# A four-layer image kernel: a feed-forward part on 32x32 tiles, a first norm per token, displaced rows of C, separate sign chains and another order of the filters

## The chip, the cores and the metric

The kernel runs on one core of one Trainium2 chip. Its time is device microseconds of one execution; the time before is the median of three executions. One further execution was profiled, and all rows of the profile come from that one.

The engines are named as in the profile: PE (TensorE; PEld its weight loads), DVE (VectorE), ACT (ScalarE), POOL (GpSimd) and SP (SyncE, which in the kernel before issues nearly every DMA; SPq is its queue). Each engine works through its own instructions in order and waits on semaphores for the others.

## The reference

Input and output are float32 images of shape (4, 64, 128, 128). Four layers follow each other:

- Layer 0: a mamba over 16,384 tokens of an image, 64 channels, 128 inner channels, 16 states, then a projection and a normalization.
- Layer 1: a windowed transform, whose windows need the sign function and an inverse of a 128x128 matrix.
- Layer 2: two 3x3 convolutions with batch norms, a gate out of means over shrinking windows, a relu.
- Layer 3: two 3x3 convolutions, then a mamba with 64 states and a feed-forward part with a depthwise 3x3 convolution over 256 hidden channels.

Layer 3 is where most of the change lies. Cut to the core:

```python
y = relu(conv2d(x, conv1_w, conv1_b))
t = tokens(conv2d(y, conv2_w, conv2_b))
t = t + mamba(layernorm(t, ln1_w, ln1_b), ...)
t = t + ffn(layernorm(t, ln2_w, ln2_b), ...)
return x + image(t)

def step(h, inp):              # in the mamba, for each token
    d_t, b_t, c_t, u_t = inp
    h = h * exp(d_t[..., None] * A) + (d_t * u_t)[..., None] * b_t[:, None, :]
    return h, einsum('bdn,bn->bd', h, c_t)

def ffn(t):
    h = t @ fc1_w.T + fc1_b                    # 64 -> 256 channels
    h = conv2d(image(h), dw_w, dw_b, groups=256)
    return gelu(tokens(h)) @ fc2_w.T + fc2_b
```

## The kernel before

The layers run one after the other, each with its own pools; images go through device memory between them. In the profiled span layer 0 lies at 0 to about 3130 us, layer 1 to about 4285, the convolutions of layers 2 and 3 to about 5090, layer 3's mamba to about 16,380 and the feed-forward part to the end.

**The mambas** (`_Mamba`, used by layer 0 and layer 3). Tokens are taken in chunks of 1024; four images of 16,384 tokens make 64 chunks. A chunk is a row of iterations, 16 in layer 0 and 64 in layer 3. An iteration holds 32 of the 128 inner channels with 4 of the states in its 128 partitions, and 1024 tokens in the free dimension; four iterations, one for each 32 channels, make a group of 4 states. ACT makes the decays `da` (L582); PE spreads B or its product over the partitions in PSUM (L514 and L520; of the second kind DVE multiplies `bx` by `du`, L526); DVE's scan (L626) runs the recurrence from `da` and `bx` into a slot of `ring`, written 8 elements after the slot's start; POOL multiplies the slot by the rows of C, `cb`, and writes it to the slot's start (L632); PE sums over the states (`y`, L457). `cb` is loaded by `_C` (L417): SyncE sends four 128 KB transfers for a group, each one row of C broadcast to 32 partitions, into a 128x1024 tile with three buffers, up to 6 iterations ahead. The tile, the slots of `ring` and the operands start at multiples of 16 bytes.

The work of a chunk that isn't an iteration is written as generators, whose steps the loop puts in at given iterations: `ahead` before the chunk (in layer 3 the centring at 41 to 43 iterations before the chunk's start, the causal convolution at 32 before), `behind` after it. The convolution takes four taps as two matmul passes (L300): the tile S holds the normalized tokens in partitions 64 to 127 and the same tokens shifted by one in partitions 0 to 63. Before, the shifted copy is made by loading it: X is read twice from `t3`, once one token earlier, and centring (PE), square and reciprocal root (ACT) and multiply (POOL, L1518) run over 128x1024, so each token is normalized twice. `tail` keeps the last two columns for the next chunk. `behind` (L1524 on) loads the tokens `tr` and the image x3 as `xr`, projects, adds `tr` to `xr` on POOL (L1537), stores the sum in `s3` and the second norm in `n3`.

**Layer 1's sign function** (L939 to L960): two matrices, km plus and minus a small multiple of the identity, go through 27 iterations of X, each X*X, a combination Z with the identity, and X*Z symmetrized. Both matrices lie beside each other in one tile: two matmuls, one DVE operation over 128x256 (L950), four matmuls, one DVE copy over 128x256 (L956). The inversion after it (L966 to L978) has one such chain alone.

**The convolutions of layers 2 and 3** (`layer2_convs3`): first all weights and the vectors of the batch norms are loaded and combined, some thirty small loads; then the first strips are loaded (`fetch`), turned on DVE and POOL (`turned`, L1214; L1218 and L1220 are POOL's two subtractions of image rows) and multiplied (`product`, L1223).

**The feed-forward part** (`layer3_ffn`). 32 strips of 16 rows of 128 pixels. The 256 hidden channels are two halves of 128: half 1 (`h1`) has its nine depthwise taps on DVE (`taps`, L1663 and L1665, each over 128x2048), half 0 (`h0`) on PE as matmuls with 64x64 diagonal matrices (L1717): four tiles at once, two row halves by two column halves, so that a step of nine handles 8 of the 16 rows, and nine steps run twice per strip. `first` is a generator: it loads N with its halo, lets POOL zero the edge columns of `h` (L1629, L1630), and three times per half runs fc1 on PE (L1638) into one PSUM tile `ph`, which ACT evacuates into `h` in two activations (L1643); it is stepped between the taps of the strip before. `second` (L1675) sums fc2 on PE into `po` and lets DVE add bias and `res` (L1684); SyncE then stores `out` (L1690). `res` is loaded by SyncE from `s3` (L1706), which already holds x + t. The DVE taps of the next strip are cut into pieces of 4, 1 and 4 between the adds.

Of the kernel before, what the change touches and what calls it, by code (L numbers as in the profile page):

```python
# [170 lines left out]
class _Mamba:  # L171
# [245 lines left out]
    def _C(self, c, g):  # L417
        t = self.t("cb", 3)
        for q in range(NQ):
            n = NQ * g + q  # L420
            self.nc.sync.dma_start(t[DD * q : DD * (q + 1)], c["C"][n : n + 1, :].to_broadcast([DD, TC]))
        return t
# [423 lines left out]
def _dual_window(tc, K, lm, nscale, r4):  # L846
# [10 lines left out]
    with ExitStack() as ctx:  # L857
# [81 lines left out]
        for a, _ in {*SIGN_STEPS, *INV_STEPS}:  # L939
            eyes[a] = cp.tile([P, 2, P], F32, name=f"eye{a}".replace(".", "_"))  # L940
            nc.vector.tensor_scalar_mul(eyes[a], K.eye.unsqueeze(1).to_broadcast([P, 2, P]), a / 2)
        X = ip.tile([P, 2, P], F32, name="X", tag="X")
        for i, sg in enumerate((tau, -tau)):
            nc.vector.scalar_tensor_tensor(X[:, i, :], K.eye, sg, km, ALU.mult, ALU.add)
        for a, b in SIGN_STEPS:
            py = pp.tile([P, 2, P], F32, name="pk", tag="pk")
            for i in range(2):
                nc.tensor.matmul(py[:, i, :], X[:, i, :], X[:, i, :], start=True, stop=True)
            Z = ip.tile([P, 2, P], F32, name="Z", tag="Z")
            nc.vector.scalar_tensor_tensor(Z, py, -b / 2, eyes[a], ALU.mult, ALU.add)  # L950
            px = pp.tile([P, 2, P], F32, name="pk", tag="pk")
            for i in range(2):
                nc.tensor.matmul(px[:, i, :], X[:, i, :], Z[:, i, :], start=True, stop=False)
                nc.tensor.matmul(px[:, i, :], Z[:, i, :], X[:, i, :], start=False, stop=True)
            X = ip.tile([P, 2, P], F32, name="X", tag="X")
            nc.vector.tensor_copy(X, px)  # L956
        pi, qi = cp.tile([P, P], F32, name="pi"), cp.tile([P, P], F32, name="qi")
        nc.vector.tensor_sub(qi, X[:, 0, :], X[:, 1, :])
# [10 lines left out]
        for a, b in INV_STEPS:  # L969
# [3 lines left out]
            nc.vector.scalar_tensor_tensor(Z, py[:, 0, :], -b / 2, eyes[a][:, 0, :], ALU.mult, ALU.add)  # L973
# [287 lines left out]
def layer2_convs3(ctx, tc, K, w, w3, x2, x3, t3):  # L1261
# [8 lines left out]
    wts = [cv.weights(cp, src, f"cw{k}") for k, src in enumerate((w["c1"], w["c2"], w3["c1"], w3["c2"]))]  # L1270
    eps = cp.tile([P, 1], F32, name="eps2")
    nc.vector.memset(eps, 1e-5)
    norms = []
    for i in "12":
        g, b, m, v, cb = (
            _dup(nc, cp, w[k], f"{k}_") for k in (f"bn{i}_g", f"bn{i}_b", f"bn{i}_m", f"bn{i}_v", f"c{i}_b")
        )
        _rstd(nc, v, v, eps)
        nc.vector.tensor_mul(g, g, v)
        nc.vector.tensor_sub(cb, cb, m)  # L1280
        nc.vector.tensor_mul(cb, cb, g)
        nc.vector.tensor_add(cb, cb, b)
        norms.append((g, cb))
    bias3 = [_dup(nc, cp, w3[k], f"{k}3") for k in ("c1_b", "c2_b")]
    eca = cp.tile([P, 3], F32, name="eca")
    nc.sync.dma_start(eca, w["eca"].to_broadcast([P, 3]))
    band = cp.tile([P, P], F32, name="band")
    nc.vector.tensor_scalar(band, K.sh0, eca[:, 0:1], None, ALU.mult)
    nc.vector.scalar_tensor_tensor(band, K.sh1, eca[:, 1:2], band, ALU.mult, ALU.add)
    nc.vector.scalar_tensor_tensor(band, K.sh2, eca[:, 2:3], band, ALU.mult, ALU.add)  # L1290

# [143 lines left out]
    fetch(2)  # L1435
    V = {0: cv.turned(source(*units[0], got[units[0]]))}
    last = None
    for n, (kind, pr, s) in enumerate(units):
        p = cv.product(V.pop(n), wts[kind])
        fetch(loads.index((kind, pr, s)) + 3 if kind in (0, 2) else 0)  # L1440
        if last is not None and kind == 0 and s == 2:
            gated(last)
            last = None
# [19 lines left out]
def layer3_mamba(ctx, tc, K, w, t3, x3, s3, n3):  # L1463
# [16 lines left out]
    tail = cp.tile([P, 2], F32, name="tail")  # L1480

    def load(c):
        b, t0 = c["at"]
        X = c["X"] = m.t("X", 1)
        if t0:
            nc.sync.dma_start(X[:64], t3[b, :, t0 - 1 : t0 - 1 + TC])
        else:
            nc.gpsimd.memset(X[:64, 0:1], 0.0)
            nc.sync.dma_start(X[:64, 1:], t3[b, :, : TC - 1])
        nc.sync.dma_start(X[64:], t3[b, :, t0 : t0 + TC])  # L1490

    def ahead(c):
# [3 lines left out]
        S = m.t("S", 1, TC + 2)  # L1496
        if t0:
            nc.gpsimd.tensor_copy(S[:, :2], tail)
        else:
            nc.gpsimd.tensor_copy(S[:, :2], pad.to_broadcast([P, 2]))  # L1500
        xs, sq = m.tmp("nxc"), m.tmp("nsq")
        yield m.slot(c, "centre")
        pm = m.take()
# [8 lines left out]
        pm = m.take()  # L1512
# [5 lines left out]
        nc.gpsimd.tensor_mul(S[:, 2:], xs, sq)  # L1518
        if not t0:
            nc.gpsimd.tensor_copy(S[:64, 2:3], pad[:64])  # L1520
        nc.gpsimd.tensor_copy(tail, S[:, TC:])
        yield from m.front(c, S, lambda: None)

    def behind(c, yg):  # L1524
        b, t0 = c["at"]
        tx = m.tmp("tx")
        tr, xr = tx[:, :512], tx[:, 512:]
        for h in range(NH):
            nc.sync.dma_start(tr[64 * h : 64 * (h + 1)], _halves(t3[b], t0)[h])
            nc.sync.dma_start(xr[64 * h : 64 * (h + 1)], _halves(x3[b], t0)[h])  # L1530
# [6 lines left out]
        nc.gpsimd.tensor_add(xr, xr, tr)  # L1537
# [17 lines left out]
        for h in range(NH):  # L1555
            nc.sync.dma_start(_halves(s3[b], t0)[h], xr[64 * h : 64 * (h + 1)])
            nc.sync.dma_start(_halves(n3[b], t0)[h], o[64 * h : 64 * (h + 1)])
# [6 lines left out]
def layer3_ffn(ctx, tc, K, w, n3, s3, out):  # L1564
# [7 lines left out]
    NK = R // 8  # L1572
    half = [slice(64 * h, 64 * (h + 1)) for h in range(2)]
    cp = ctx.enter_context(tc.tile_pool(name="ffc", bufs=1))
    wp = ctx.enter_context(tc.tile_pool(name="ffw", bufs=2))
    hp = ctx.enter_context(tc.tile_pool(name="ffp", bufs=1, space=PSUM))
    dp = ctx.enter_context(tc.tile_pool(name="ffd", bufs=2, space=PSUM))
# [3 lines left out]
    f2 = cp.tile([P, 64], F32, name="f2")  # L1581
    nc.sync.dma_start(f2, w["fc2_wT"][P:, :])

    f2h = cp.tile([P, 2, 64], F32, name="f2h")
    dwb = cp.tile([P, 2], F32, name="dwb")
    dww = cp.tile([P, 2, 9], F32, name="dww")
    diag = cp.tile([P, 9, 64], F32, name="diag")
    for h in range(2):
        nc.sync.dma_start(f1[half[h]], w["fc1_wT"].rearrange("c (t q) -> c t q", t=2))
        nc.sync.dma_start(f2h[half[h]], w["fc2_wT"][:P, :].rearrange("(i q) c -> q i c", i=2))  # L1590
        nc.sync.dma_start(dwb[half[h]], w["dw_b"][:P, :].rearrange("(i q) o -> q (i o)", i=2))
    b1 = cp.tile([P, 2], F32, name="ff_fc1_b")
    nc.sync.dma_start(b1, w["fc1_b"].rearrange("(t q) o -> q (t o)", t=2))

    g, n = (_dup(nc, cp, w[k], f"ff_{k}") for k in ("ln2_w", "ln2_b"))
# [5 lines left out]
    dwb1 = cp.tile([P, 1], F32, name="dwb1")  # L1601
    nc.sync.dma_start(dwb1, w["dw_b"][P:, :])
    nc.sync.dma_start(dww, w["dw_w"].rearrange("(t q) k -> q t k", t=2))
    for k in range(9):
        for h in range(2):
            nc.vector.tensor_scalar(
                diag[half[h], k, :], K.eye[half[h], half[h]], dww[half[h], 0, k : k + 1], None, ALU.mult
            )
    b2 = _dup(nc, cp, w["fc2_b"], "fc2b_")

    def first(b, r0, H):


        nimg = n3[b].rearrange("c (r w) -> c r w", w=WW)
        N = wp.tile([P, HR, WW], F32, name="N", tag="N")
        rng = []
        if r0 == 0:
            nc.vector.memset(N[:64, 0:1, :], 0.0)
        if r0 + R == HH:
            nc.vector.memset(N[64:, HR - 1 : HR, :], 0.0)  # L1620
# [5 lines left out]
        yield  # L1626
# [24 lines left out]
    strips = [(b, r0) for b in range(B) for r0 in range(0, HH, R)]  # L1651
    H = {}
    for _ in first(*strips[0], H):
        pass

    def taps(h1):

        g1 = wp.tile([P, R, WW], F32, name="g1", tag="g1")
        for k in range(9):
# [6 lines left out]
            yield g1  # L1666

    def more(gen, n):
        for _ in range(n):
            g = next(gen, None)  # L1670
        return g

    def second(n, g0, g1, res, o, kk):

        b, r0 = strips[n]  # L1675
        po = op.tile([P, 2, 4, WW], F32, name="po", tag="po")
        for h in range(2):
            r = 8 * kk + 4 * h
            nc.tensor.matmul(po[half[h], h], f2, g1[:, r : r + 4, :], start=True, stop=False)  # L1679
        for i in range(2):  # L1680
            for h in range(2):
                nc.tensor.matmul(po[half[h], h], f2h[half[h], i, :], g0[i][half[h], kk], start=False, stop=i == 1)  # L1682
        for h in range(2):
            nc.vector.scalar_tensor_tensor(  # L1684
                o[half[h], kk], po[half[h], h], b2[half[h]], res[half[h], kk], ALU.add, ALU.add
            )
        if kk == NK - 1:
            oimg = out[b].rearrange("c (r w) -> c r w", w=WW)
            for q in range(R // 4):
                nc.sync.dma_start(oimg[:, r0 + 4 * q : r0 + 4 * q + 4, :], o[half[q % 2], q // 2])  # L1690

    pin = _Pin(tc)
    g1 = more(taps(H[1]), 9)
    rest, owed = iter(()), None
    for n, (b, r0) in enumerate(strips):
# [3 lines left out]
        ahead = first(*strips[n + 1], H) if n + 1 < len(strips) else iter(())  # L1701
        next(ahead, None)

        res = wp.tile([P, NK, 4, WW], F32, name="res3", tag="res3")
        for q in range(R // 4):
# [136 lines left out]
```

## Time and profile before

| | us |
|---|---|
| median of three executions | 17,327.41 (17,321.47 to 17,331.91) |
| profiled execution | 17,333.11 |
| its span | 17,331.3 |
| PE busy in the span | 13,927.6 (80%) |
| DVE | 15,802.2 (91%) |
| ACT | 14,324.0 (83%) |
| POOL | 14,169.2 (82%) |
| mean granted TensorE clock | 0.909 |

Busy shares are means over stages with different limits, so each stage has to be read by itself. A row of the groups names the line, the engine, the operation, output and input tiles with their partitions and elements, the count, then busy time and mean ns of one, then the engine's idle time just before these instructions and what ended it. A row of the timeline has start and length, and in brackets the idle time before and who ended it. A row of the waits has engine, line, whom it waited for, us in all, times, longest.

### The profile page before, as it was taken

The numbers are of one execution on the slowest core, as the hardware profiler recorded it, in microseconds if no ns is written. First come the engines' busy times: TensorE is split into PE (matmuls) and PEld (weight loads), VectorE is DVE, ScalarE is ACT, GpSimd is POOL, SyncE is SP. The second block draws the span as 40 slices with busy tenths as digits, with TensorE's granted clock in tenths as the row PEclk, the third lists the DMA queues.
The fourth block names the chain that finished last, engine by engine and source line by source line (L and its number), as shares of the span: only waits on it lengthen the run. The fifth ranks groups of instructions, "written<-read, shape, count | busy, mean of one in ns | idle before, by whom it ended". The sixth has DMA issues, their size and how long they took to land. (4 is left out here: it accounts for less than half of the span.)

```text
span 17331.3 us, 238151 instructions
## 1 busy us (share of the span) xinstructions
PE 13927.6 (80%) x79418; PEld 6901.8 (40%) x79418; DVE 15802.2 (91%) x9155; ACT 14324.0 (83%) x29905; POOL 14169.2 (82%) x8290
## 2 busy tenths in 40 slices
PE   7888888788987777777777777777777777777799
PEld 3333333388443333333333333333333333333333
DVE  8999999622879999999999999999999999999887
ACT  8999999211539999999999999999999999999733
POOL 7999999301439999999999999999999999999700
PEclk8888888789989999999999999999999999999899
DMA  6666666211343333333333333333333333333222
GB/s 161 178 177 178 178 178 178 74 42 51 130 129 83 96 83 95 84 94 87 89 90 89 90 88 91 87 93 87 91 88 92 86 93 83 96 84 96 66 57 55
DMA packets 684405, 1761.99 MB, mean 102 GB/s; under 512 B 197712, under 2 KB 241696, under 8 KB 673696
## 3 DMA queue, kind: packets, MB, share of 16 engines
q1 hardware_dynamic: 683168, 1746.75, 37.0%
q8 instruction: 623, 10.21, 0.2%
q14 instruction: 614, 5.03, 0.1%
HBM read 1456.61 MB, written 289.41 MB: 101 GB/s over the span
## 5 line engine op out<-in xcount | busy, mean ns | idle before, releaser
L632 POOL TENSOR_TENSOR ring<-ring,cb 128x1024 f32<-128x1024 f32 x5120 | 12031.7, 2378 | 334.2 <-DVE ring L626 180.2
L626 DVE TENSOR_TENSOR_SCAN ring<-da,state,bx 128x1024 f32<-128x1024 f32 x4848 | 11054.9, 2329 | 68.5 <-PE y L457 38.3
L431 ACT ACTIVATE bxT<-duT,BT 128x128 f32<-128x128 f32 x21504 | 6705.6, 389 | 31.5 <-PE bx L514 28.9
L582 ACT ACTIVATE da<-dl,A 128x1024 f32<-128x1024 f32 x5120 | 5750.5, 1139 | 166.5 <-DVE ring L626 112.9
L514 PE MATMUL bx<-cst,bxT 128*128 128x128 f32 x24576 | 3691.6, 300 | 943.7 <-DVE ring L626 644.8
L514 PEld LDWEIGHTS bx<-cst,bxT 128*128 128x128 f32 x24576 | 3244.7, 209 | 2342.8 <-DVE ring L626 1536.1
L520 PE MATMUL bx<-bc,spread 64*128 64x512 f32 (+1 forms) x8192 | 2405.1, 684 | 1439.6 <-DVE ring L626 1428.9
L457 PE MATMUL y<-ring,cst 128*32 128x512 f32 x20480 | 3017.9, 673 | 118.4 <-POOL ring L632 117.3
L526 DVE TENSOR_TENSOR bx<-du,bx 128x1024 f32<-128x1024 f32 x2048 | 2465.4, 1212 | 303.9 <-PE bx L520 184.2
L520 PEld LDWEIGHTS bx<-bc,spread 64*128 64x128 f32 (+1 forms) x8192 | 690.2, 195 | 2821.6 <-DVE ring L626 2307.1
L457 PEld LDWEIGHTS y<-ring,cst 128*32 128x32 f32 x20480 | 632.1, 119 | 2035.5 <-issue 1437.5
L300 PE MATMUL bx<-S,cw 128*128 128x512 f32 x1024 | 671.1, 815 | 368.4 <-DVE ring L626 355.1
L435 POOL TENSOR_TENSOR bxT<-duT,BT 128x512 f32<-128x512 f32 x768 | 805.0, 1048 | 9.9 <-ACT BT L381 9.9
L1232 PE MATMUL m<-V,cw 64*64 64x512 f32 x6144 | 713.3, 603 | 101.2 <-POOL V L1218 67.4
L1122 POOL TENSOR_TENSOR xs<-xs,cl 128x1024 f32<-128x1024 f32 x32 | 75.9, 2371 | 858.2 <-DVE cl L1121 858.2
L1629 POOL MEMSET h<- 128x18 f32 x64 | 8.3, 131 | 875.2 <-PE pd L1717 443.5
L1643 ACT ACTIVATE h<-ph,ff_fc_b 128x384 f32<-128x384 f32 (+1 forms) x384 | 200.8, 577 | 593.3 <-PE ph L1638 575.7
L1717 PE MATMUL pd<-h,diag 64*64 64x512 f32 x4608 | 631.8, 602 | 0.7 <-issue 0.7
L1663 DVE SCALAR_TENSOR_TENSOR g<-h,dww,g 128x2048 f32<-128x2048 f32 x256 | 602.0, 2351 | 11.4 <-DVE g L1663 0.5
L626 DVE TENSOR_TENSOR_SCAN ring<-da,bx 128x1024 f32<-128x1024 f32 x272 | 604.8, 2270 | 6.7 <-PE y L457 3.4
L300 PEld LDWEIGHTS bx<-S,cw 128*128 128x128 f32 x1024 | 256.0, 263 | 787.5 <-DVE ring L626 464.8
L1232 PEld LDWEIGHTS m<-V,cw 64*64 64x64 f32 x6144 | 355.0, 136 | 457.6 <-issue 273.9
(340 smaller groups left out, 10591.7 us busy)
## 6 DMA issues: line engine op xcount, KB each, us to landing
cb<-c SPq DMA_DIRECT2D x5120, 128.0 KB, 2.8
dl<-d SPq DMA_DIRECT2D x2048, 128.0 KB, 3.2
du<-d SPq DMA_DIRECT2D x2048, 128.0 KB, 3.6
d<-pos SPq DMA_DIRECT2D x128, 512.0 KB, 3.7
d<-u SPq DMA_DIRECT2D x128, 512.0 KB, 3.8
X<-d_t SPq DMA_DIRECT2D x124, 256.0 KB, 4.1
S<-in_x SPq DMA_DIRECT2D x120, 256.5 KB, 4.5
res<-in_x SPq DMA_DIRECT2D x128, 128.0 KB, 2.9
```

Source lines behind the costliest of these rows:

```text
L300: self.nc.tensor.matmul(out[: l.shape[1], k : k + 512], l, r[:, k : k + 512], start=i == 0, stop=i == len(pairs) - 1)
L431: nc.scalar.activation(t[:, k, q].rearrange("p e j -> p (e j)"), c["duT"][:, k, :], AF.Copy, scale=c["BT"][:, k, n : n + 1])
L435: nc.gpsimd.tensor_mul(t[:, k].rearrange("p q e j -> p q (e j)"), c["duT"][:, k].unsqueeze(1).to_broadcast(shape), c["BT"][:, k, NQ * g : ...
L457: nc.tensor.matmul(c["y"][DD * j : DD * (j + 1), _COLS[h]], K.sel, hc[:, _COLS[h]], start=False, stop=u["g"] == self.ng - 1,)
L514: nc.tensor.transpose(bx[:, P * m : P * (m + 1)], v["bxT"][:, m, :, :, j].rearrange("p q e -> p (q e)"), self.K.eye)
L520: nc.tensor.matmul(bx[:, _COLS[h]], self.spread[v["g"]][r], self.rows(v["c"]["B"], h, 0), start=True, stop=True)
L526: nc.vector.tensor_mul(tiles[k], v["c"]["du"][j], tiles[k])
L582: nc.scalar.activation(das[nexp], v["c"]["dl"][k], AF.Exp, scale=self.A[:, k, v["g"] : v["g"] + 1])
L626: nc.vector.tensor_tensor_scan(hs, das.pop(i), tiles[i], 0.0 if u["c"].get("reset") else st, ALU.mult, ALU.add)
L632: nc.gpsimd.tensor_mul(hc, hs, u["cb"])
L1232: self.nc.tensor.matmul(p[k][i][half[h]], U[half[i], k, x, :], V[half[i], k, NP * h : NP * (h + 1), x : x + WW], start=x == 0, stop=x == 2,)
L1717: nc.tensor.matmul(pd[i][half[h]], diag[half[i], k, :], h0[half[i], r : r + 4, dx : dx + WW], start=k == 0, stop=k == 8,)
```

## The change

Five parts:

1. Feed-forward part. The depthwise matmuls of half 0 use 32x32 diagonal tiles, sixteen at a time (row group r times quarter q of the strip), so that one round of nine steps covers all 16 rows. For that PSUM has four tiles `pd`; quarter q of the rows has the four channel groups rotated by q groups of 32 partitions, with `f2r` and `dwb` as four rotated copies of the weights. The nine DVE taps of the next strip are issued in one run, before the adds of the strip before; the adds go over 128 partitions. N is loaded two strips ahead, with its halo zeroed by POOL. x3 is no longer added in the mamba: SyncE loads `res` from `s3`, and four DMAs issued by POOL add x3 to it (`accum_op`), before the edge memsets of the next strip in program order.
2. First norm once per token (layer 3's mamba). X holds 1024 tokens as two halves of 512 in the 128 partitions; centring, square, root and multiply run over 128x512; four SBUF-to-SBUF DMAs per chunk write the result into S, once plain and once shifted by one, two loop slots after the multiply; `tail` holds three columns. `behind` no longer loads x3 and adds it.
3. `cb` gets two elements more, and the rows of C start 8 bytes behind the tile's start, in both mambas.
4. Sign chains: the two matrices have their own tiles in SBUF and PSUM; each has its own DVE step for Z; one's copy is on DVE, the other's on ACT.
5. Layer 2: weights of the first convolution, then the first strips; the other filters' loads, the batch norms and the band matrix are made in `ready`, called after the first product. A call of `gated` on `last`, which was always None, is dropped.

The diff, cut to its core:

```diff
     def _C(self, c, g):
-        t = self.t("cb", 3)
+        t = self.t("cb", 3, TC + 2)[:, 2:]
...
         for a, b in SIGN_STEPS:
-            py = pp.tile([P, 2, P], F32, name="pk", tag="pk")
+            py = [pp.tile([P, P], F32, name=f"py{i}", tag=f"py{i}", bufs=1) for i in range(2)]
+            px = [pp.tile([P, P], F32, name=f"px{i}", tag=f"px{i}", bufs=1) for i in range(2)]
+            Z = [ip.tile([P, P], F32, name=f"Z{i}", tag=f"Z{i}") for i in range(2)]
             for i in range(2):
-                nc.tensor.matmul(py[:, i, :], X[:, i, :], X[:, i, :], start=True, stop=True)
-            nc.vector.scalar_tensor_tensor(Z, py, -b / 2, eyes[a], ALU.mult, ALU.add)
+                nc.tensor.matmul(py[i], X[i], X[i], start=True, stop=True)
+                nc.vector.scalar_tensor_tensor(Z[i], py[i], -b / 2, eyes[a], ALU.mult, ALU.add)
             for i in range(2):
-                nc.tensor.matmul(px[:, i, :], X[:, i, :], Z[:, i, :], start=True, stop=False)
-                nc.tensor.matmul(px[:, i, :], Z[:, i, :], X[:, i, :], start=False, stop=True)
-            nc.vector.tensor_copy(X, px)
+                nc.tensor.matmul(px[i], X[i], Z[i], start=True, stop=False)
+                nc.tensor.matmul(px[i], Z[i], X[i], start=False, stop=True)
+            nc.vector.tensor_copy(X[0], px[0])
+            nc.scalar.copy(X[1], px[1])
...
     fetch(2)
+    wts = [cv.weights(cp, w["c1"], "cw0")]
     V = {0: cv.turned(source(*units[0], got[units[0]]))}
     for n, (kind, pr, s) in enumerate(units):
         p = cv.product(V.pop(n), wts[kind])
         fetch(loads.index((kind, pr, s)) + 3 if kind in (0, 2) else 0)
+        if not n:
+            ready()
...
     def ahead(c):
-        S = m.t("S", 1, TC + 2)
-        xs, sq = m.tmp("nxc"), m.tmp("nsq")
+        S = m.t("S", 1, TC + 3)
+        no = m.tmp("nx")
+        xs, sq = no[:, :512], no[:, 512:]
...
-        nc.gpsimd.tensor_mul(S[:, 2:], xs, sq)
-        if not t0:
-            nc.gpsimd.tensor_copy(S[:64, 2:3], pad[:64])
-        nc.gpsimd.tensor_copy(tail, S[:, TC:])
+        nc.gpsimd.tensor_mul(xs, xs, sq)
+        nc.gpsimd.tensor_copy(S[:, :3], tail if t0 else pad.to_broadcast([P, 3]))
+        for h in range(2):
+            nc.gpsimd.tensor_copy(tail[64 * h : 64 * (h + 1), : 3 - h], xs[64:, 509 + h :])
+        yield "next", 0
+        yield "next", 0
+        for k in range(2):
+            for h in range(NH):
+                at = 3 - k + 512 * h
+                nc.sync.dma_start(S[64 * k : 64 * (k + 1), at : at + 512], xs[64 * h : 64 * (h + 1)])
...
     def behind(c, yg):
         for h in range(NH):
             nc.sync.dma_start(tr[64 * h : 64 * (h + 1)], _halves(t3[b], t0)[h])
-            nc.sync.dma_start(xr[64 * h : 64 * (h + 1)], _halves(x3[b], t0)[h])
...
-        nc.gpsimd.tensor_add(xr, xr, tr)
...
+        load(n + 2)
+        ahead = first(n + 1, H)
+        res = wp.tile([P, 2, 4, WW], F32, name="res3", tag="res3", bufs=3)
+        ximg = x3[b].rearrange("c (r w) -> c r w", w=WW)
+        for eng, img, add in ((nc.sync, simg, ALU.bypass), (nc.gpsimd, ximg, ALU.add)):
+            for q in range(R // 4):
+                eng.dma_start(res[half[q % 2], q // 2], img[:, r0 + 4 * q : r0 + 4 * q + 4, :], accum_op=add)
+        g0 = [wp.tile([P, 4, WW], F32, name=f"g0{q}", tag=f"g0{q}") for q in range(NR)]
+        o = wp.tile([P, 2, 4, WW], F32, name="o3", tag="o3")
+        pd = [dp.tile([P, 4, WW], F32, name=f"pd{q}", tag=f"pd{q}") for q in range(NR)]
+        for k in range(9):
+            dy, dx = divmod(k, 3)
+            for q in range(NR):
+                for r in range(NR):
+                    nc.tensor.matmul(
+                        pd[q][quad[(r + q) % NR]],
+                        diag[quad[r], k, :],
+                        h0[quad[r], 4 * q + dy : 4 * q + dy + 4, dx : dx + WW],
+                        start=k == 0,
+                        stop=k == 8,
+                    )
+            if k in (0, 1, 2, 4, 5, 6):
+                next(ahead, None)
+            if k == 2 and 1 in H:
+                g2 = taps(H[1])
+            pin()
+        nc.scalar.activation(g1, g1, AF.Gelu, bias=dwb1)
+        for q in range(NR):
+            nc.scalar.activation(g0[q], pd[q], AF.Gelu, bias=dwb[:, q : q + 1])
+        if owed:
+            second(*owed)
+        pin()
+        owed, g1 = (n, g0, g1, res, o), g2
```

`second` after the change:

```python
def second(m, g0, g1, res, o):
    b, r0 = strips[m]
    po = op.tile([P, 2, 4, WW], F32, name="po", tag="po")
    for q in range(NR):
        nc.tensor.matmul(po[half[q % 2], q // 2], f2, g1[:, 4 * q : 4 * q + 4, :], start=True, stop=False)
    for q in range(NR):
        nc.tensor.matmul(po[half[q % 2], q // 2], f2r[:, q, :], g0[q], start=False, stop=True)
    oimg = out[b].rearrange("c (r w) -> c r w", w=WW)
    for kk in range(2):
        nc.vector.scalar_tensor_tensor(o[:, kk], po[:, kk], b2, res[:, kk], ALU.add, ALU.add)
        for h in range(2):
            r = r0 + 8 * kk + 4 * h
            nc.sync.dma_start(oimg[:, r : r + 4, :], o[half[h], kk])
```

## The prediction

> **What bounds the kernel now.** First I read the busy time by stretches of the span, one stretch inside layer 0, one inside layer 3's mamba, one inside the feed-forward part (columns: window, its length, busy us of PE, PEld, DVE, ACT, POOL, granted clock, DMA share, GB/s):
>
> ```profile
> 500.00:3000.00 2500.00, 2109.95 (x11186) 975.39 (x11187) 2431.54 (x1309) 2347.35 (x4550) 2335.39 (x1308) 0.90 0.69 178
> 6000.00:16000.00 10000.00, 7724.89 (x42562) 3780.54 (x42563) 9837.38 (x5091) 9478.01 (x20769) 9657.41 (x5497) 0.92 0.33 89
> 16400.00:17200.00 800.00, 782.10 (x5260) 240.37 (x5260) 642.66 (x366) 287.64 (x473) 11.98 (x120) 0.98 0.23 56
> ```
>
> Both mambas are bound by DVE (97.3% and 98.4%), with POOL close behind; the feed-forward part is bound by PE (98%), with DVE at 80%. Next, what DVE's idle 163 us of the mamba stretch wait for:
>
> ```profile
> DVE bx L526 <- PE bx L520: 108.2, 117, 1.4
> DVE ring L626 <- PE y L457: 37.0, 68, 1.1
> DVE ring L626 <- PE bx L514: 5.0, 21, 0.6
> ```
>
> Then the rows of POOL, shapes kept apart (count, then busy us and mean ns):
>
> ```profile
> L632 POOL TENSOR_TENSOR ring<-ring,cb 128x1024 f32<-128x1024 f32 x5120 | 12031.7, 2378 | 334.2 <-DVE ring L626 180.2 <-issue 94.0 <-DMA cb<-c 58.3
> L1220 POOL TENSOR_TENSOR V<-X 128x1040 f32<-128x1040 f32 x32 | 96.3, 3010 | 0.0
> L1218 POOL TENSOR_TENSOR V<-X 128x1040 f32<-128x1040 f32 x32 | 66.6, 2081 | 153.7 <-PE m L1232 73.4 <-ACT X L1341 54.3 <-DMA X<-d_x 22.7
> L811 POOL TENSOR_TENSOR m<-h 128x2048 f32<-128x2048 f32 x16 | 61.4, 3843 | 36.9 <-DVE h L808 36.9
> ```
>
> L1218 reads two rows 520 bytes apart (8 beyond a multiple of 16), L1220 rows 1040 apart (a multiple of 16), L811 rows shifted by 4 bytes. The shifted pairs cost 2.0 and 1.88 ns an element, ring L632 2.32 and L1220 2.89.
>
> Last, the timeline of the feed-forward part: SyncE's queue, DVE's taps of the first strip, and ACT's evacuations of its fc1 (start, length, what, idle before):
>
> ```profile
> 16698.10 13.39 SPq L1690 DMA_DIRECT2D out<-o  x4
> 16711.58 1.20 SPq L1625 DMA_DIRECT2D N<-d_n  x2
> 16712.83 2.50 SPq L1706 DMA_DIRECT2D res<-d_s  x4
> ...
> 16406.10 1.29 DVE L1665 TENSOR_SCALAR g<-h,dww 128x2048 f32<-128x2048 f32 x1 [8.05 <-ACT h L1643]
> 16407.42 19.06 DVE L1663 SCALAR_TENSOR_TENSOR g<-h,dww,g 128x2048 f32<-128x2048 f32 x8
> ...
> 16399.44 0.94 ACT L1643 ACTIVATE h<-ph,ff_fc_b 128x256 f32<-128x256 f32 x2 [17.60 <-DMA N<-d_n]
> 16402.13 1.05 ACT L1643 ACTIVATE h<-ph,ff_fc_b 128x384 f32<-128x384 f32 x2 [1.75 <-PE ph L1638]
> 16404.94 1.05 ACT L1643 ACTIVATE h<-ph,ff_fc_b 128x384 f32<-128x384 f32 x2 [1.75 <-PE ph L1638]
> ```
>
> SyncE works in order, some 0.62 us an issue, and sat 13.39 us at an output store that waits for DVE's add: a load queued behind the stores goes out only after that add. One strip's nine taps hold DVE 20.35 us; three evacuations, each behind its matmuls, take 6.55 us from the first's start to the third's end.
>
> **Feed-forward part, +310 us.** The 64x64 depthwise matmuls (L1717) become 32x32 ones, four row and four column tiles at once. The trace has no such tile. A strip has 288 records of 512 columns as before (144 matmuls, each recorded as two passes). Now twelve groups of 24 take 2.74 us each, 114 ns a record with four tiles at work. With sixteen at work the floor is a quarter, 28 ns; if every record must be issued at the present pace, it is 114 ns. I take half of that, 57: a step of the tap loop (32 records) then takes 1.8 us, about as long as the evacuation and its wait beside which it runs, and PE isn't the bound. [...]
>
> With PE away, DVE would need 20.35 + 1.53 us (two adds) a strip, 21.9 against the 28 of now. But the change moves x3's addition into four accumulating DMAs issued by POOL, each behind SyncE's load of the same quarter of res. In POOL's queue they stand ahead of the memsets of the next strip's h, and ACT's first evacuation of that h, and so DVE's taps, wait for these memsets. SyncE's loads of res stand behind the output stores, which wait for the adds, which stand in DVE's order behind the taps. That closes a ring, in which nothing overlaps:
> taps 20.35; adds 1.53; the first pair of stores sticks out by 0.51 (1.28 of issue less an add of 0.77); second pair 1.28; N 1.20; res 2.50; landing of the last res, 4.1 from issue, 3.5 left over; POOL's four issues and the memsets 2.4; evacuations 6.55. Sum 39.8 us a strip.
> The POOL term: no row shows a DMA issued by POOL. From below it is one of its memsets, 0.13 us; from above its nearest full pass, 2.38. I take 1.0, as SyncE's issue of the same transfer costs 0.62 and lies nearer the low end. Four of these, started as the loads land 0.62 apart, end 2.1 after the last landing, and two memsets add 0.26.
> Landing may be as short as the stores' 2.3 us. So the ring lies between 36.0 (2.3 landing, 0.13 issue) and 45.4 (2.38 issue).
>
> The stage: the mamba's last stores go out at 16378; eleven more small weight loads (27 for 16) at 0.62 us put the first tap at 16412.9. The ring first binds for the fourth strip, as the first two adds come late: two taps of some 21.5 bring the third to 16456, then 29 links of 39.8 to 17610, then 20.35 of taps, 2.0 gelu, some 4 of output matmuls, 1.53 adds, 3.6 store: 17641 against 17331, +310 (bounds +200 and +472).
>
> **The displaced rows of C and norm once, -95 us.** The L3 mamba has 4096 multiplies L632. By L1218's and L811's rates I expect 1.9 to 2.05 us for 2.378, which leaves POOL some 20 us a chunk of 175. Norm once halves ACT's centre, square and rstd, halves POOL's S multiply (2.417 for 1024 elements), and drops the addition L1537 (1.288); it adds three small POOL copies and four SBUF-to-SBUF DMAs, issued two slots after the multiply and some five before the convolution, against landings of 4.5 us and slots of 2.7. None of this is on DVE, so the gain is only DVE's waiting for POOL. Following single gaps back, PE's y L457 waits for ring L632 in all of the 37 us and about half of the 108; the rest is the convolution L300 holding PE, which stays. 37 + 54 + 5 = 96 of 10,000, over 11,240 some 108, of which I take 95. Ends: 0, and all of DVE's idle, 183.
> In layer 0 (1024 multiplies) POOL also becomes faster, but DVE's only wait is 51 us in 2500 for PE's bx L520, none for y: nothing.
>
> [...]
>
> **Sign chains, -38 us.** 27 iterations at the granted clock of 0.54:
>
> ```profile
> 3480.30 0.42 DVE L956 COPY X<-pk 128x256 f32<-128x256 f32 x1 [2.17 <-PE pk L954]
> 3484.64 0.42 DVE L956 COPY X<-pk 128x256 f32<-128x256 f32 x1 [2.17 <-PE pk L954]
> ...
> 3500.69 0.80 PE L971 MATMUL pk<-A 128*128 128x128 f32 x2 [0.17 <-DVE A L967]
> 3503.48 0.80 PE L971 MATMUL pk<-Xi,A 128*128 128x128 f32 x2 [0.38 <-DVE Xi L978]
> ```
>
> A pair now takes 4.34 us; one such chain alone, the inversion, 2.79. In own tiles one chain's DVE step lies beside the other's matmuls. PE's twelve passes 0.21 apart fill 2.5 us. I take 2.9: 27 x 1.43 = 38. Ends: 50 (PE's 2.5 alone) and 20 (3.6, if the chains get in each other's way).
>
> **Filters in another order, -6 us.** The first X of layer 2 is issued at 4317, behind some thirty small loads; it can go some 15 us sooner, but the norm's vectors then stand in DVE's order ahead of the second source, and their loads end at about the same time. 0 to -15.
>
> **Sum:** 310 - 95 - 38 - 6 = +171 on the profiled execution of 17,333.1 us (span 17,331.3): 17,504. The median shown lies 6 below it: 17,498.
>
> **Rivals.**
> A, the ring doesn't bind (faster). If POOL's DMAs and SyncE's loads run ahead of the taps, DVE bounds: the stage ends at 16412.9 + 32 x 21.9 + 11 = 17,125, 206 sooner; with the other 139 that is -345, 16,982. For it: DMA is busy 23% and POOL 1.5%. Against it: the orders above. It decides from 33.9 us a strip (171 / 29 less than 39.8): there the whole change comes out even.
> B, the multiply stays at 2.38 us, as S L1518 does, whose output alone is displaced (2417 ns): no 95, 17,593. For it: the shifted rows are other operations, some beside DVE's.
> C, the tiles are bound by issue, or POOL's DMAs cost 2.4: steps of 3.6 us stretch each of three evacuation rounds by about 2, as the dear issue does the ring by 5.6: +160, 17,660.
>
> **How the numbers follow.** Forecast 0.60, A 0.15, B 0.13, C 0.12. The range leaves out A and the last of C: from 17,300 (ring 36, mamba -180) to 17,720. A measurement tells 0.2%, 35 us. Slower: B, C and all but 0.08 of the forecast, 0.77; of those 0.08, same 0.04; faster 0.04 and A, 0.19.
>
> **What would show it.** Taps L1665 start some 39 to 40 us apart, ahead of each a DVE gap of some 18 us released by ACT h, whose own gap ends at POOL's memset; SyncE waits for the adds. Ring L632 shows 1.9 to 2.05 us, and DVE's wait for y is gone. The pairs of the sign chain come 2.9 apart. It is wrong if taps start 22 apart (A), or if L632 stays.

## The result and the profile after

| | before | after |
|---|---|---|
| median, us | 17,329.4 (20 runs, 17,321.5 to 17,334.9) | 17,303.0 (20 runs, 17,297.1 to 17,308.2) |
| span of the profiled execution, us | 17,331.3 | 17,306.3 |

Ratio 0.9985, 95% interval 0.9978 to 0.9991: 26 us faster, where 17,498, 169 us slower, was forecast. The stages follow each other, so their shares can be read off the two traces, from DVE's first and last scan of each mamba:

| stage | before, us | after, us | difference | forecast |
|---|---|---|---|---|
| layer 0 | 3136.3 | 3135.4 | -0.9 | 0 |
| layers 1 and 2, convolutions of layer 3 | 2048.3 | 1966.4 | -81.9 | -44 |
| mamba of layer 3 | 11,183.8 | 11,112.0 | -71.8 | -95 |
| feed-forward part | 962.9 | 1092.5 | +129.6 | +310 |

So three stages gain 155 us, and the feed-forward part gives most of it back. That part did get slower and its strip is a ring, but a shorter one than forecast. First the busy times of the same three kinds of stretches as before (layer 0, mamba, feed-forward; window, length, busy us of PE, PEld, DVE, ACT, POOL, clock, DMA share, GB/s):

```profile
500.00:3000.00 2500.00, 2110.11 (x11183) 960.51 (x11181) 2427.96 (x1310) 2347.34 (x4551) 2043.97 (x1311) 0.86 0.69 178
6000.00:16000.00 10000.00, 7631.51 (x42604) 3738.83 (x42604) 9875.65 (x5122) 9437.21 (x20892) 8339.75 (x5530) 0.91 0.33 90
16300.00:17200.00 900.00, 619.87 (x8940) 179.62 (x8940) 574.87 (x295) 290.72 (x466) 108.61 (x230) 0.83 0.32 66
```

In the mambas POOL is no longer close behind DVE (82 and 83% for 97 and 99%), and DVE is still not full. POOL's row of the multiply, over the whole span (count, busy us, mean ns), shows why:

```profile
L632 POOL TENSOR_TENSOR ring<-ring,cb 128x1024 f32<-128x1024 f32 x5120 | 10232.2, 2009 | 2071.9 <-DVE ring L626 1656.0 <-issue 265.5 <-PE bx L514 61.9
```

In the feed-forward part nobody is full any more: PE 69%, DVE 64%. Now its timeline, a strip and a bit, DVE, ACT, POOL and SyncE:

```profile
16630.69 1.29 DVE L1675 TENSOR_SCALAR g<-h,dww 128x2048 f32<-128x2048 f32 x1 [11.52 <-POOL h L1644]
16632.01 19.13 DVE L1673 SCALAR_TENSOR_TENSOR g<-h,dww,g 128x2048 f32<-128x2048 f32 x8
16651.06 1.41 DVE L1688 SCALAR_TENSOR_TENSOR o<-po,fc2b__119136,res 128x512 f32<-128x512 f32 x2
16663.97 1.29 DVE L1675 TENSOR_SCALAR g<-h,dww 128x2048 f32<-128x2048 f32 x1 [11.51 <-POOL h L1644]
...
16634.55 1.05 ACT L1658 ACTIVATE h<-ph,ff_fc_b 128x384 f32<-128x384 f32 x2 [12.37 <-PE ph L1653]
...
16660.49 3.31 POOL L1713 DMA_DIRECT2D res<-d_x  x4 [29.70 <-DMA res<-d_s]
16662.57 1.37 POOL L1644 MEMSET h<- 128x18 f32 x1
...
16651.83 2.41 SPq L1691 DMA_DIRECT2D out<-o  x4
16654.34 1.18 SPq L1632 DMA_DIRECT2D N<-d_n  x2
16655.70 2.38 SPq L1713 DMA_DIRECT2D res<-d_s  x4
```

Read it as a chain: taps end at 16651.14, adds, stores from 16651.83, N, loads of res at 16655.70, POOL's DMAs from 16660.49 to 16663.80 behind 29.70 us of waiting for those loads, memset, taps at 16663.97, at once. The evacuations are not in it. Those at 16634.55 belong to the strip after; the taps that start at 16630.69 use an `h` evacuated one round earlier and wait for the edge memsets alone. The distance of the taps is 33.28 us.

### The profile page after: what moved, and what is told of

Its sections match the earlier page's. It is cut to its first block, busy times and chain, and to the rows that moved or that the text cites. A ratio compares the mean times of both kernels' runs of the same rounds, so it can differ in the third digit from the quotient of the medians.

```text
span 17306.3 us, 246894 instructions
## 1 busy us (share of the span) xinstructions
PE 13549.5 (78%) x83514; PEld 6698.5 (39%) x83514; DVE 15706.0 (91%) x9103; ACT 14222.8 (82%) x29932; POOL 12385.2 (72%) x8418
## 4 chain that ended last, share of the span: by engine, by line
DVE 34%; issue 19%; PE 6%; ACT 5%; DMA 4%; SPq 3%; POOL 1%; DVEq 0%; POOLq 0%; ACTq 0%
DVE ring L626 23%; DVE bx L526 8%; DVE g L1673 3%; PE bx L300 2%; ACT bxT L431 2%; DMA dl<-d 2%; ACT da L582 2%; SPq L553 2%; PE m L1233 1%; DMA cb<-c 1%; PE bx L514 1%; DMA res<-d_s 1%; DMA du<-d 1%; PE y L457 1%; PE bx L520 1%
## 5 line engine op out<-in xcount | busy, mean ns | idle before, releaser
L632 POOL TENSOR_TENSOR ring<-ring,cb 128x1024 f32<-128x1024 f32 x5120 | 10232.2, 2009 | 2071.9 <-DVE ring L626 1656.0
L457 PE MATMUL y<-ring,cst 128*32 128x512 f32 x20480 | 2855.9, 680 | 4.7 <-POOL ring L632 4.7
L457 PEld LDWEIGHTS y<-ring,cst 128*32 128x32 f32 x20480 | 586.2, 120 | 1775.1 <-issue 1702.0
L300 PE MATMUL bx<-S,cw 128*128 128x512 f32 x1024 | 759.9, 909 | 337.0 <-DVE ring L626 323.6
L1713 POOL DMA_DIRECT2D res<-d_x x128 | 106.5, 1258 | 922.5 <-DMA res<-d_s 921.3
L300 PEld LDWEIGHTS bx<-S,cw 128*128 128x128 f32 x1024 | 289.3, 297 | 803.4 <-DVE ring L626 433.6
L1722 PE MATMUL pd<-h,diag 32*32 32x512 f32 x9216 | 376.8, 671 | 188.9 <-POOL h L1645 161.2
```

The lines of the kernel that those rows point to most:

```text
L300: self.nc.tensor.matmul(out[: l.shape[1], k : k + 512], l, r[:, k : k + 512], start=i == 0, stop=i == len(pairs) - 1)
L457: nc.tensor.matmul(c["y"][DD * j : DD * (j + 1), _COLS[h]], K.sel, hc[:, _COLS[h]], start=False, stop=u["g"] == self.ng - 1,)
L632: nc.gpsimd.tensor_mul(hc, hs, u["cb"])
```

## The experiments

Twelve further kernels follow. Unless said otherwise they are the changed kernel with one edit. The feed-forward part first.

**Edge memsets ahead of the accumulating DMAs.** `first` is split, and the part that allocates `h` and clears its edges is called before `res` is loaded:

```diff
+        edges(n + 1, H)
         ahead = first(n + 1, H)
         res = wp.tile([P, 2, 4, WW], F32, name="res3", tag="res3", bufs=3)
```

> The changed kernel, with POOL's edge memsets of the next strip issued ahead of the four accumulating DMAs instead of behind them; everything else as it is. Theory (the ring through POOL's queue, adds - stores - loads of res - POOL's DMAs - memsets - taps, sets the strip): the taps no longer wait for POOL, the distance of their starts falls from 33.3 us to DVE's own 21.9 to 22.5, the feed-forward part from 1092 to about 765 us, the time to about 16,980. Rival (behind the ring PE and ACT need nearly as long, since PE has some 21 us of work a strip and waits for two engines): the distance falls only to 26 to 28 us, the time to 17,090 to 17,150.

Measured: 16,962.1 us, ratio to the kernel before 0.9789 (0.9774 to 0.9804). The taps on DVE's timeline:

```profile
16615.32 1.28 DVE L1682 TENSOR_SCALAR g<-h,dww 128x2048 f32<-128x2048 f32 x1
16616.64 19.13 DVE L1680 SCALAR_TENSOR_TENSOR g<-h,dww,g 128x2048 f32<-128x2048 f32 x8
16635.69 1.40 DVE L1695 SCALAR_TENSOR_TENSOR o<-po,fc2b__119136,res 128x512 f32<-128x512 f32 x2
16637.01 1.28 DVE L1682 TENSOR_SCALAR g<-h,dww 128x2048 f32<-128x2048 f32 x1
```

No bracket: DVE has no idle time left, 21.7 us a strip, and the feed-forward part takes 751.8 us for 1092.5. The ring was the only cause; PE and ACT keep up.

**The evacuations made to wait.** The edge memsets are two columns wide, so they overlap what ACT writes afterwards.

```diff
-            nc.gpsimd.memset(himg[:, :, 0:1], 0.0)
-            nc.gpsimd.memset(himg[:, :, RW - 1 : RW], 0.0)
+            nc.gpsimd.memset(himg[:, :, 0:2], 0.0)
+            nc.gpsimd.memset(himg[:, :, RW - 2 : RW], 0.0)
```

> The changed kernel, with the edge memsets two columns wide, so that ACT's evacuations overlap them and must wait for them, as the prediction wrongly had it. Theory (the only wrong term of the predicted 39.8 us was the 6.55 us of evacuations, because these run ahead of the memsets): the distance of the taps' starts goes from 33.3 to about 39.8 us, the time to about 17,490. Rival (the terms were wrong in several places and 33.3 came by accident; the evacuations would be hidden by the other strip's work anyway): distance within 1 us of 33.3, time within 30 us of 17,303.

Measured: 17,511.4 us (ratio 1.0105, 1.0088 to 1.0122), taps 40.8 apart (median of the strips). Two taps on DVE, and the first of the evacuations on ACT that the second one needs:

```profile
16615.79 1.29 DVE L1675 TENSOR_SCALAR g<-h,dww 128x2048 f32<-128x2048 f32 x1 [18.98 <-ACT h L1658]
16656.65 1.29 DVE L1675 TENSOR_SCALAR g<-h,dww 128x2048 f32<-128x2048 f32 x1 [19.08 <-ACT h L1658]
...
16649.28 1.05 ACT L1658 ACTIVATE h<-ph,ff_fc_b 128x384 f32<-128x384 f32 x2 [22.04 <-POOL h L1645]
```

The gap is released by ACT, and ACT's own gap by POOL's memset, as the prediction had drawn it, and the strip is within 1 us of the predicted 39.8. With the dependency that the prediction assumed, its ring comes out; the real kernel doesn't have that dependency.

**The ring cut elsewhere.** SyncE issues a strip's loads of res one strip earlier (`residual(n + 1)` allocates the tile and loads it from `s3`, as was done for strip n); POOL's order stays.

```diff
+        residual(n + 1)
+        res = R3.pop(n)
-        for eng, img, add in ((nc.sync, simg, ALU.bypass), (nc.gpsimd, ximg, ALU.add)):
-            for q in range(R // 4):
-                eng.dma_start(res[half[q % 2], q // 2], img[:, r0 + 4 * q : r0 + 4 * q + 4, :], accum_op=add)
+        for q in range(R // 4):
+            nc.gpsimd.dma_start(res[half[q % 2], q // 2], ximg[:, r0 + 4 * q : r0 + 4 * q + 4, :], accum_op=ALU.add)
```

> The changed kernel with the ring cut at another place: POOL's order stays (accumulating DMAs ahead of the memsets), but SyncE issues a strip's loads of res one strip earlier, ahead of the stores that wait for the adds. Theory (it is a ring, so any one link taken out opens it): the taps start 21.7 to 22.5 us apart as with the memsets moved, the time 16,960 to 16,985. Rival (the accumulating DMAs themselves hold POOL, or contend, so that only the order on POOL helps): the distance stays above 26 us.

Measured: 16,960.8 us (0.9788, 0.9771 to 0.9804), taps 21.68 apart. POOL still issues its four DMAs ahead of the memsets and still waits for the loads:

```profile
16624.35 3.31 POOL L1723 DMA_DIRECT2D res<-d_x  x4 [18.90 <-DMA res<-d_s]
```

It costs nothing any more. These loads still stand behind the stores of the adds, but the memsets that follow them now serve the taps after the next: the same chain spans two strips, and half of its 33 us is less than DVE's 21.7. Of the links of this ring two were changed, each alone, and each takes it out.

**The rows of C back at the tile's start.** `t = self.t("cb", 3)`.

> The changed kernel with the rows of C back at the tile's start. Theory (the displacement makes POOL's multiply faster, and that is what took DVE's waits for POOL out of the L3 mamba): the multiply is back at 2.37 to 2.38 us, the L3 mamba gets 40 to 70 us longer, the time 17,345 to 17,375. Rival (norm once, which takes work off POOL and ACT, did it): the multiply is back but the mamba stays within 15 us.

Measured: 17,301.8 us (17,261.4 to 17,314.2 over ten runs). The multiply is back at 2378 ns and the mamba not longer: 11,100.9 us, 11 less, in a kernel whose runs spread over 53 us. The theory falls: with norm once in place, and the rest as it is, the displacement brings nothing.

**Displaced by 16 bytes.** `t = self.t("cb", 3, TC + 4)[:, 4:]`.

> The changed kernel with the rows of C displaced by 16 bytes instead of 8. Theory (what counts is the distance of the two operands within 16 bytes): the multiply takes 2.37 to 2.38 us, as without displacement, and the time is that of the kernel with C back. Rival (any displacement does it, for instance by other buffers' addresses): 2.0 us, time as the changed kernel.

Measured: the multiply takes 2378 ns, the time is 17,309.4. Of the three displacements run, 0, 8 and 16 bytes, only 8 makes it 2009; that the buffers behind it move too isn't the reason, since they move with 16 as well.

**The displacement alone, in the kernel before.**

> The kernel before with the rows of C displaced by 8 bytes and nothing else. Undoing this part in the changed kernel left the L3 mamba 11 us shorter, not longer. Theory (faster multiply and norm once are two remedies for one and the same wait of DVE for POOL; either alone takes it out): the multiply takes 2.01 us, DVE's waits for y go, the L3 mamba falls from 11,184 to 11,110 to 11,140 us. Rival (the faster multiply helps DVE nowhere, only norm once does): L3 mamba within 15 us of 11,184.

Measured: 17,267.4 us (0.9963, 0.9949 to 0.9978), L3 mamba 11,124 us, 60 less. The mamba's length came as expected, the waits did not. DVE's waits in the window 6000 to 16,000 (who for whom, us, times, longest):

```profile
DVE ring L626 <- PE y L457: 59.8, 60, 1.4
DVE bx L526 <- PE bx L520: 47.2, 62, 1.1
```

Before it was 37.0 and 108.2. So the faster multiply takes out half of the waits for bx, and the ones for y grow to one per chunk; norm once takes out those for y. They are two waits more than one, and each part alone gains 60 and (by the kernel with C back) 83 us. Together they gain 72. Something eats the rest, and the waits of the changed kernel say where:

```profile
DVE bx L526 <- PE bx L520: 117.6, 64, 2.2
```

Nearly all of DVE's idle time, 117.6 of 124 us in this window, is one wait a chunk, of up to 2.2 us, behind the convolution L300. Its passes, grouped over the chunks between 5300 and 16,000 us of each trace:

| kernel | convolutions over 5.5 us: count, length, DVE's wait | the others |
|---|---|---|
| before | 0 | 61: 4.97 us, 0.71 |
| displacement alone | 0 | 61: 5.24, 0.81 |
| changed | 51: 6.63, 2.19 | 11: 5.40, 0.98 |
| changed, C back | 38: 6.67, 2.23 | 24: 5.16, 0.82 |

The 4.97 us of the kernel before are a mean: 15 of the 61 take 3.70 us, the others 5.1 to 5.4. PE's timeline around a long one, in the changed kernel:

```profile
10049.53 1.13 PE L520 MATMUL bx<-bc,spread 64*128 64x512 f32 x4 [1.56 <-DVE ring L626]
10052.90 6.67 PE L300 MATMUL bx<-S,cw 128*128 128x512 f32 x8 [2.24 <-DVE ring L626]
```

Pauses of 1.56 and 2.24 us, with 1.13 us of work between, and then eight passes 0.85 us apart. The next two experiments ask whether it is the clock.

**The spreading matmuls run twice, in PE's pause before the convolution.** The same values into the same tile, in one iteration of a chunk:

```diff
+                    for _ in range(2 if self.slots["conv"] == -32 and i % 64 == 32 else 1):
                         nc.tensor.matmul(bx[:, _COLS[h]], self.spread[v["g"]][r], self.rows(v["c"]["B"], h, 0), start=True, stop=True)
```

> The changed kernel; in layer 3's mamba, in the one iteration of a chunk that ends with the causal convolution, PE runs its two matmuls that spread B (L520) a second time into the same tile, with the same values, in the 2.2 us in which it then waits for DVE anyway. In the changed kernel the convolution's eight passes take 6.6 us in 51 of 62 chunks (0.85 each) and 5.4 in the others, and DVE stands 2.2 us behind the long ones, 1.0 behind the short ones; before, all took 5.0. Theory (the long ones run at half the clock, because norm once and the faster multiply have left PE pauses before them): with the pause cut to about 1.1 us most convolutions take 4.9 to 5.4 us, DVE's wait falls below 1 us a chunk, the L3 mamba from 11,112 to 11,040 to 11,070 us. Rival (the passes are slow for their operands' sake, S being written by DMA in four pieces or lying elsewhere): 6.6 us as before, L3 mamba within 10 us.

Measured: 17,209.3 us (ratio to before 0.9931, 0.9914 to 0.9948), 94 below the changed kernel, for work that is thrown away. L3 mamba 11,019 us.

```profile
10003.64 2.00 PE L521 MATMUL bx<-bc,spread 64*128 64x512 f32 x8 [1.56 <-DVE ring L627]
10007.01 3.70 PE L300 MATMUL bx<-S,cw 128*128 128x512 f32 x8 [1.38 <-DVE ring L627]
```

All 62 convolutions of the window take 3.70 us, for 4.97 on average in the kernel before and 4.9 to 5.4 expected, and DVE's wait behind them is gone: it is busy for 9975 of 10,000 us. The rival falls, as S is written by the same four DMAs. The granted clock over a convolution, third from the end, goes with its length. First one of 6.67 and one of 5.40 us in the changed kernel, then the one above:

```profile
10052.90:10059.57 6.67, 6.67 (x10) 2.59 (x10) 5.56 (x3) 4.23 (x8) 4.95 (x3) 0.55 0.24 65
7968.83:7974.23 5.40, 5.40 (x10) 2.08 (x10) 5.40 (x3) 5.37 (x10) 4.34 (x3) 0.68 0.35 99
```

```profile
10007.01:10010.71 3.70, 3.70 (x10) 1.50 (x10) 3.70 (x3) 3.68 (x8) 2.22 (x2) 1.00 0.46 125
```

The traces before and after also hold what the length goes with. In their clock records, 1094 and 1202 of them, the clock is either full or half, and changes only on a grid of 3.41 us, within 0.03 us over the whole execution. Over each of the 51 long convolutions of the changed kernel it is low in two steps, for 5.4 to 6.0 us of the passes, over each of the 11 others in one, for 3.41; in the run with the pause filled, over the one shown, in none. In the changed kernel, the long ones start 0.8 to 1.4 us after a step of the grid and the others 2.3 to 3.4, without exception, and the pauses ahead of them are nearly the same, 1.44 to 1.57 and 2.18 to 2.24 us. Most of the long ones keep their place: 35 of the 61 distances from one convolution to the next are 174.08 us within 0.05, which is 51 steps. No run moved a convolution along the grid on purpose.

**The spreading matmuls three times in all.**

> As the one before, with the two matmuls run three times in all, which fills the 2.2 us to the end. Theory: no convolution at half the clock, 4.9 us each, L3 mamba 11,030 to 11,060 us, unless the longer row delays DVE's next multiply by some tenths. Rival: 6.6 us, and the L3 mamba gets longer by up to 1 us a chunk.

Measured: 17,262.2 us. The convolutions again take 3.70 us, but the longer row ends too late and DVE waits 0.6 us a chunk for its next bx: L3 mamba 11,058 us, in a profiled execution of 17,246 us. A filler has to fit into the pause.

**The sign chains alone, in the kernel before.**

> The kernel before with the sign chains alone changed. In the changed kernel a pair of chains takes 2.0 us for 4.33, at a granted clock of 0.97 for 0.50. Theory (all of it is this part): the stretch of 27 iterations falls from 117 to about 55 us, the time by 60, to about 17,270; layer 2's first product follows the end of layer 1 by the same 41 us as before. Rival (the other parts, or a clock that other work had raised, share in it): the period stays above 2.7 us and the gain below 45.

Measured: 17,266.1 us (0.9964, 0.9951 to 0.9977), 62 less. From the last transform of layer 1 to the first product of layer 2 it is 41.6 us, as before; in the changed kernel it is 22.6, so that is the filters' part. The stretch of the 27 iterations, in the kernel before and then in the changed one (clock third from the end):

```profile
3368.50:3485.10 116.60, 85.16 (x310) 70.50 (x310) 25.72 (x72) 2.21 (x11) 0.00 (x0) 0.50 0.00 0
```

```profile
3378.80:3433.00 54.20, 50.58 (x320) 42.16 (x320) 23.28 (x80) 6.89 (x26) 0.00 (x0) 0.97 0.00 1
```

The period falls from 4.33 to 2.0 us and the clock goes from 0.50 to 0.97.

**The paired chains with idle work for PE, in the kernel before.** Eight matmuls of identity by identity an iteration, into an unused PSUM tile.

> The kernel before, its paired chains as they were, with eight further 128x128 matmuls an iteration (identity by identity into an unused PSUM tile): four behind the first two matmuls, four behind the last four, where PE waits for DVE. 216 matmuls more in all. Theory (a good half of the chains' gain comes of the clock, which is granted where PE doesn't pause): the granted clock in the stretch goes from 0.50 to over 0.9 and the period from 4.33 to 2.9 to 3.2 us, though more is computed. Rival (it is all overlap of one chain with the other, the clock follows from something else): the clock stays and the period grows to 4.6 to 5.5 us.

Measured: 17,290.7 us (0.9978, 0.9968 to 0.9988), 38 less, for 216 matmuls more. Many of them stand earlier in PE's order than their iteration, so that they ended at 3430, while iterations went on without them. Busy times and clock, with fillers, without, and after the chains:

```profile
3386.00:3410.00 24.00, 24.00 (x201) 23.36 (x199) 7.22 (x17) 0.00 (x0) 0.00 (x0) 1.00 0.00 1
...
3430.00:3463.00 33.00, 21.14 (x134) 16.94 (x132) 10.00 (x27) 0.00 (x0) 0.00 (x0) 0.97 0.00 1
3463.00:3560.00 97.00, 65.48 (x233) 50.95 (x233) 21.37 (x54) 1.01 (x1) 0.00 (x0) 0.55 0.24 100
```

The period is 2.91 us with them and without. That is of use: from 3430 on the same instructions, with the same pauses of 0.5 us, run at 0.97 which before ran at 0.50. Half the clock isn't the price of the pauses alone: in this profile it is gone behind the burst of fillers. Of the chains' 2.33 us an iteration, 1.42 are the clock (4.33 to 2.91); 0.91 are left for what own tiles change, the overlap and the shorter DVE steps together, which no run separates.

**Both corrections.** Edge memsets first and C back:

> The changed kernel with both corrections: edge memsets ahead of the accumulating DMAs, and the rows of C back at the tile's start. Theory (norm once alone takes out DVE's waits for POOL, and the displacement beside it costs the L3 mamba some 11 us): taps 21.7 us apart, L3 mamba about 11,100 us, the time about 16,950. Rival (those 11 us were scatter): L3 mamba at 11,112 and the time at 16,962.

Measured: 16,946.9 us, but spread from 16,930 to 16,964 over four runs; L3 mamba 11,071.5 in its profile, with 13 long convolutions. The median lies near the 16,950 of the theory, but by neither theory: with norm once and C aligned the number of long convolutions differs from profile to profile (38 with C back, 35 with 16 bytes, 13 here), and the mamba's time goes with it.

Edge memsets first, C displaced, and the spreading matmuls twice:

> The changed kernel with the edge memsets ahead of the accumulating DMAs (measured 16,962) and the two matmuls run once more before the convolution (measured 17,209, 94 below the changed kernel). The two lie in stages that follow each other, so by the theory the gains add: 16,962 - 94 = 16,868, with the taps 21.7 us apart and the L3 mamba at about 11,020 us. Rival (the mamba's gain hangs on the state in which a run happens to be): L3 mamba above 11,050, the time above 16,900.

Measured: 16,868.5 us (five runs, 16,866.6 to 16,869.8), ratio to the kernel before 0.9734 (0.9721 to 0.9747); L3 mamba 11,018.9 us. It is faster than both kernels by over 430 us, steady, and at the sum of the two gains.

## Why the prediction was wrong, point by point

**The ring, +310 forecast, +130 measured: the step that failed.** The prediction says that "ACT's first evacuation of that h, and so DVE's taps, wait for these memsets". The evacuation doesn't: memsets and evacuations write different columns of `h` and are ordered only by the buffer, so ACT works one strip ahead, and only the reader of both, the taps (and PE for the other half), waits. The term "evacuations 6.55" has no place in the ring. The others were right. From the start of the loads of res to the taps 8.4 us were summed and 8.27 measured (16655.70 to 16663.97); POOL's four DMAs took 3.31 us, 0.83 each for the 1.0 taken. 39.8 less 6.55 is 33.25, and 33.28 was measured. Over 29 links the term is 190 us, more than the whole forecast loss: without it the sum is -19 and the time 17,308. That this is within 5 us of the 17,303 measured is luck: it forecasts the feed-forward part 10 us too short, the mamba 23 too short, and layers 1 and 2 with layer 3's convolutions 38 too long. The run with wide memsets shows the term itself.

**The 32x32 tiles** were sized safely. A step of 32 records takes 1.14 us at full clock, 36 ns a record, between the estimated floor of 28 and the 57 taken:

```profile
16637.17 1.14 PE L1722 MATMUL pd<-h,diag 32*32 32x512 f32 x32
```

**Rival A** names the right price on the wrong condition. It gave 16,982 where POOL runs ahead; with one call moved, 16,962 was measured, and the feed-forward part gained 211 us on the kernel before, for 206. Rivals B and C fall: the multiply takes 2009 ns, a step 1.14 us and a DMA of POOL's 0.83.

**The displaced rows and norm once, -95 forecast, -72 measured.** The multiply came at 2009 ns, inside the 1.9 to 2.05 forecast. Over the mamba, DVE's waits of over 0.15 us that don't stand behind the convolution fell from 125 to 3 us, more than the 108 that the prediction counted. What was left out is what PE does with the time: its pauses before the convolution got the passes from 0.6 us to 0.85 in 51 of 62 chunks, and DVE's waits behind the convolution grew from 45 to 125 us. That leaves 43 us. Most of the other 29 is DVE's busy time, 27 us shorter (11,004 to 10,977 us); the prediction put that at nothing ("None of this is on DVE"), and no run says where it comes from. That the gain hangs on the multiply, so that without it there is "no 95" (rival B), fell too: with the multiply at 2378 ns the kernel with C back still gains 83 us, and the displacement by itself 60.
2009 against 2378 ns for the same operation, with one operand moved by 8 bytes, shows that the place of its operands counts here.

**The sign chains, -38 forecast, -62 measured**, beyond the end of 50. That end was worked out at a granted clock of 0.54, as if that were a property of the stage. It belongs to the kernel: PE's 12 passes go from 0.21 to 0.11 us apart. The mechanism was right, the clock was the mis-sized term.
The burst of fillers shows too that it isn't the stage's (1.00 under it and 0.97 behind it, 0.50 without). In the mamba the clock was at half for 5.4 to 6.0 of the passes' 6.4 to 6.7 us in 51 of 62 chunks, behind a pause of 2.24 us with one of 1.56 shortly before, and full (1.00) in the convolution shown where the second was 1.38.

**The filters, -6 forecast**, some -11 measured for layer 2 (first product 19.0 us sooner after layer 1, 7.6 lost again behind it), and 5 to 6 more up to the first scan; some 4 us of layer 1 are left without an owner. Layer 0 came as forecast, nothing.

## What to carry to other kernels

A wait found in the order of two instructions is not yet a dependency: write down which bytes each of them writes, since a ring is as long as its true dependencies and one wrong link per strip weighs more than all prices together. Move small clears and other short work ahead of instructions that wait for transfers on the same queue. And when an engine that was late becomes early, look at the clock of the one that now pauses: work thrown away in the pause gained 94 us here.

## What the runs showed of the hardware

- POOL's multiply L632 of 128x1024 float32 takes 2378 ns where its two operands lie equally within 16 bytes (before, and in the changed kernel with C back or displaced by 16), and 2009 ns where they lie 8 bytes apart.
- In the clock records of the traces before and after, the granted clock is full or half and changes only on a grid of 3.41 us. Eight passes of 512 columns (L300) take 3.70 us at full clock (15 of 61 before), 5.1 to 5.4 with one step at half (the other 46, and 11 of 62 after) and 6.4 to 6.7 under two (51 of 62 after).
- After pauses of PE of some 1.56 and 2.24 us, in the changed kernel, the length goes with the place of the passes' start in that grid: 0.8 to 1.4 us after a step they took 6.4 to 6.7 us, 2.3 to 3.4 us after it 5.40. With the second pause cut to 1.38 us all 62 took 3.70. In the kernel before, with pauses of 0.9 to 1.3 and 2.7 us, the 15 that start 1.5 to 1.8 us after a step have none at half, and the 46 that start at 0.4 to 0.5 or 2.1 to 3.1 have one.
- The same chain of small matmuls with pauses of 0.5 us ran at a granted clock of 0.50 in the kernel before, and at 0.97 behind a burst of fillers.
- In the changed kernel thirty-two 32x32 records of 512 columns, for sixteen tiles, take 1.14 us at full clock; at half clock 2.0. Four accumulating DMAs of 128 KB take POOL 3.31 us, 0.83 each, behind loads issued 0.6 us apart, and land 4.2 us after their issue.
